# Expert stages with slot tiles of two 64-slot parts, the second part's weights copied by VectorE

## The chip, the cores and the metric

The kernel runs on one core of one Trainium2 chip. The metric is device microseconds of one launch; three runs of the kernel before took 2853.52, 2857.5 and 2858.4 us, median 2857.5 us. The engines are written as in the profile: PE is TensorE (PEld its weight loads), DVE is VectorE, ACT is ScalarE, POOL is GpSimd, SP is SyncE. A q behind a name (DVEq) is that engine's sequencer, which reads registers, waits on semaphores, branches and issues transfers.

## What is computed

One sequence of 1024 tokens with 512 features goes through six layers. Everything is float32. Each layer adds its result to x after a layer norm:

```
x = x + 0.5 * expert_ffn(ln(x))     # expert stage f0
x = x + attention(ln(x))            # 32 heads, causal
x = x + 0.5 * expert_ffn(ln(x))     # expert stage f1, same weights
x = x + 0.5 * lora_ffn(ln(x))
x = x + mamba(ln(x))
x = x + 0.5 * lora_ffn(ln(x))
```

The change lies in the two expert stages:

```
logits = x @ W_gate + b_gate                     # 8 experts
_, top_idx = top_k(logits, 2)
y_all = relu(einsum('bsd,edh->bseh', x, W_e) + b_e)   # W_e: 8 x 512 x 512
y = take_along_axis(y_all, top_idx[..., None], axis=2).mean(axis=2)
```

Only the two chosen experts of each token are needed, so there are 2048 pairs of token and expert per stage.

## The kernel before, in words

`expert_ffn` is called twice, with the tag f0 (ahead of attention) and f1 (behind it). It sorts the 2048 pairs by expert into slots. A slot tile is 128 slots of one expert; an expert's number of pairs is rounded up to whole tiles, so 16 tiles are always needed (NS0) and 23 at most (NS). The steps are these.

- Routing. The layer norm, the gate and the two best experts of each token are found, then ranks within each expert, the number of tiles per expert (`nt`, lines 458 to 467), the slot of each pair (`pos`), and, by small bf16 matmuls (line 526), the token of each slot (`token`) and the expert of each tile (`of_i`, line 592).
- Tiles. `gather(s)` (line 547) is an indirect transfer on POOL's queue: it fetches the 128 token rows of tile s from DRAM into `xs`. `turn(s)` (line 181) transposes them on PE by four 128x128 transposes and copies the result to `xt` on ACT (line 564). `slot_tile(s)` first turns tile s + 1, then multiplies tile s: four matmuls of 128 rows, 128 columns and 512 moving columns into one PSUM bank (line 608). The moving operand is the expert's 512x512 weight in `w_all`, picked by a register (`ep` on PE, `ev` on DVE) that is loaded from `of_i` (lines 604, 605). In float32 each matmul appears in the trace as two passes with a weight load each. DVE adds the bias (line 616), ACT applies the ReLU and the factor (line 622), and ACT's queue stores the tile to `outs` (line 623).
- The last tiles. Tiles 0 to 15 stand in straight code. Tiles 16 and up stand in nested `If(n > s)` blocks (line 649), where n is the real number of tiles, read into registers of PE, DVE, ACT and SP. Instructions are ordered by a scheduler within a block of straight code, and are not moved out of an `If` block.
- Collecting. POOL gathers the two result rows of each token from `outs` (line 666), and DVE adds them to x (line 695). It waits until all tiles are stored.

The buffers that matter: `xs`, `xt` and `y` have 3 buffers each, rows of late tiles come from a pool of 4 (`more_rows`), and PSUM tiles rotate through 4 banks (`psml`).

In f0 the weights come from DRAM while routing runs: experts 0 to 3 at once, 4 and 5 behind the fourth row store, the biases and experts 6 and 7 behind the second gather (`hold` puts a small POOL memset ahead of a transfer, so that the transfer waits for POOL's queue). POOL also runs six preparing products of the attention weights in f0 (lines 793 and 818), each queued behind one of the gathers of tiles 11 and up.

Of the kernel before, what the change touches and what calls it, by code (L numbers as in the profile page):

```python
# [22 lines left out]
P = 128  # L23
S = 1024
D = 512
NT = S // P
KT = D // P
# [5 lines left out]
HG = 4  # L33

NE = 8
NS = 2 * S // P + NE - 1
NS0 = 2 * S // P
NE1 = 4
RANK = 8
# [37 lines left out]
def macaron_kernel(  # L77
# [23 lines left out]
    nc = tc.nc  # L101
# [48 lines left out]
    def queue_behind(ins, prev):  # L150

        tc.add_manual_dep(
            ins.ins,
            prev.ins.name,
            mybir.DependencyInfo(mybir.DependencyClass.NoSync, mybir.DependencyReason.DATA),
            reason="queue_behind",
        )
        return ins

    def hold(w):  # L160

        tc.keep_in_program_order(nc.gpsimd.memset(w, 0.0))
# [166 lines left out]
    def gate_steps(keep=store_rows, own=None):  # L329
        return (  # L330
            lambda t: normalize(t, keep, own=own),
            transpose_h,
            None,
            lambda t: narrow_by_columns(t, gate_w, NE),
            gates,
        )

    def expert_ffn(tag, meanwhile, behind_weights=lambda: None):
# [4 lines left out]

        with tc.tile_pool(name=f"{tag}wa", bufs=1) as wap, tc.tile_pool(
            name=f"{tag}r", bufs=1
        ) as rp, tc.tile_pool(name=f"{tag}m", bufs=4) as more_rows, tc.tile_pool(name=f"{tag}w", bufs=3) as wk:
            w_all = wap.tile([P, NE, KT, D], F32, tag="w_all", name="w_all")
            b_all = wap.tile([P, NE, D], F32, tag="b_all", name="b_all")

            def load_expert(e):  # L350
                return nc.sync.dma_start(
                    w_all[:, e, :, :], w_e[e].rearrange("(k p) c -> p k c", p=P)
                )

            def load_biases():
                return nc.sync.dma_start(
                    b_all.rearrange("p e c -> p (e c)"),
                    b_e.rearrange("e c -> (e c)").partition_broadcast(P),
                )

            def gates_of_input():


                def keep(t, xn):
                    tc.keep_in_program_order(
                        nc.sync.dma_start(rows[t * P : (t + 1) * P, :], xn)
                    )
                    if t == 3:
                        for e in range(4, 6):
                            tc.keep_in_program_order(load_expert(e))  # L370

                def own(t):
                    return wk.tile([P, D], F32, tag=("xs", "xt", "y")[t % 3], name="xn_own")

                for e in range(4):
                    load_expert(e)
                Tiles(*gate_steps(keep, own)).flush()
# [8 lines left out]
            lanes = rp.tile([P, P], F32, tag="lanes", name="lanes")  # L386
            steps = rp.tile([P, NS + 1], F32, tag="steps", name="steps")
            counts = rp.tile([P, P], I32, tag="counts", name="counts")
            nc.gpsimd.iota(counts, pattern=[[1, P]], base=0, channel_multiplier=0)
            nc.gpsimd.tensor_copy(lanes, counts)  # L390
            nc.gpsimd.tensor_scalar(steps, lanes[:, : NS + 1], float(P), None, ALU.mult)

            over = rp.tile([P, NT], F32, tag="over", name="over")
            nc.gpsimd.tensor_copy(over, steps[:, :NT])
            nc.gpsimd.memset(over[:, 0:1], -1.0)
            bounds = rp.tile([P, NE + 1], F32, tag="bounds", name="bounds")
            nc.gpsimd.memset(bounds, 0.0)
# [12 lines left out]
            by_e = [P, NE, NT]  # L410
# [4 lines left out]
            if tag == "f0":  # L415
# [22 lines left out]
            ps = psml.tile([P, 512], F32, tag="ps", name="ps_rank")  # L438
            ne = NT * NE
# [5 lines left out]
                lhsT=ones_b,  # L445
                rhs=sums.rearrange("p e t -> p (e t)"),
                start=True,
                stop=False,
# [3 lines left out]
                lhsT=at_most_b,  # L452
                rhs=both.rearrange("p e t -> p (e t)"),
                start=False,
                stop=True,
            )
            more = rp.tile(by_e, F32, tag="more", name="more")
            nc.vector.tensor_tensor(
                more,
                ps[:, ne : ne + NE].unsqueeze(2).to_broadcast(by_e),  # L460
                over.unsqueeze(1).to_broadcast(by_e),
                ALU.is_gt,
            )
            nt = rp.tile([P, NE], F32, tag="nt", name="n_tiles")
            nc.vector.tensor_reduce(nt, more, AX.X, ALU.add)
            base, ends = bounds[:, :NE], bounds[:, 1:]
            nc.vector.tensor_tensor_scan(
# [3 lines left out]
            nc.vector.scalar_tensor_tensor(  # L471
                at,
                base.unsqueeze(1).to_broadcast([P, NT, NE]),
                float(P),
                ps[:, :ne].rearrange("p (e t) -> p t e", t=NT),
                ALU.mult,
                ALU.add,
# [11 lines left out]
            flat = pos.rearrange("p i t -> p (i t)")  # L489
            past = rp.tile([P, n2, NS + 1], BF16, tag="past", name="past_s")  # L490
            nc.vector.tensor_tensor(
                past,
                flat.unsqueeze(2).to_broadcast([P, n2, NS + 1]),
                steps.unsqueeze(1).to_broadcast([P, n2, NS + 1]),
                ALU.is_ge,
# [20 lines left out]
            ps = psml.tile([P, 512], F32, tag="ps", name="ps_slot")  # L516
            for j in range(n2):
                if j % 4 == 0:
# [48 lines left out]
            for s in range(2):  # L567
                gather(s)
            if tag == "f0":

                hold(b_all[0:1, :, 0:1])
                hold(w_all[0:1, 6:, 0, 0:1])
                tc.keep_in_program_order(load_biases())
                for e in range(6, NE):
                    tc.keep_in_program_order(load_expert(e))


            past = rp.tile([P, NS, NE], F32, tag="past_e", name="past")
            queue_behind(
                nc.vector.tensor_tensor(  # L580
                    past,
                    ends.unsqueeze(1).to_broadcast([P, NS, NE]),
                    lanes[:, :NS].unsqueeze(2).to_broadcast([P, NS, NE]),
                    ALU.is_le,
                ),
                known,
            )
            of = rp.tile([P, NS], F32, tag="of", name="of_f")
            nc.vector.tensor_reduce(of, past, AX.X, ALU.add)
            nc.vector.tensor_scalar(of, of, float(NE - 1), None, ALU.min)  # L590
            of_i = rp.tile([P, NS], I32, tag="of_i", name="of_i")
            nc.vector.tensor_copy(of_i, of)
            for i in range(2):
                queue_behind(nc.vector.tensor_copy(slot[i], pos[:, i, :]), known)
# [4 lines left out]
            def slot_tile(s):  # L599
                if s + 1 < NS:  # L600
                    turn(s + 1)
                xt = turned.pop(s)
                low, high = max(0, s - (NS - NE)), min(s, NE - 1)
                ep = nc.tensor.value_load(of_i[0:1, s : s + 1], min_val=low, max_val=high)
                ev = nc.vector.value_load(of_i[0:1, s : s + 1], min_val=low, max_val=high)
                ps = psml.tile([P, 512], F32, tag="ps", name="ps_e")
                for k in range(KT):
                    nc.tensor.matmul(
                        ps,
                        lhsT=xt[:, k, :],  # L610
                        rhs=w_all[:, bass.ds(ep, 1), k, :].rearrange("p e c -> p (e c)"),
                        start=(k == 0),
                        stop=(k == KT - 1),
                    )
                y = wk.tile([P, D], F32, tag="y", name="y_e")
                nc.vector.tensor_tensor(
                    y,
                    ps,
                    b_all[:, bass.ds(ev, 1), :].rearrange("p e c -> p (e c)"),
                    ALU.add,  # L620
                )
                nc.scalar.activation(y, y, AF.Relu, scale=0.25)
                nc.scalar.dma_start(outs[s * P : (s + 1) * P, :], y)

# [24 lines left out]
            with ExitStack() as more_tiles:  # L649
                n = nc.values_load(  # L650
                    n_i[0:1, :],
                    engines=[mybir.EngineType.PE, mybir.EngineType.DVE, mybir.EngineType.Activation, mybir.EngineType.SP],
                    min_val=NS0,
                    max_val=NS,
                )
                for s in range(NS0, NS):
                    more_tiles.enter_context(tc.If(n > s))
                    slot_tile(s)

    pairs = {}  # L660
# [910 lines left out]
    with tc.tile_pool(name="left", bufs=1) as left:  # L1571
        first, later = {}, []
# [67 lines left out]
```

## Time and profile before

| what | value |
|---|---|
| median of three runs | 2857.5 us |
| profiled execution: time, span | 2855.43 us, 2853.7 us |
| PE, DVE, ACT, POOL busy | 97%, 61%, 25%, 32% of the span |
| granted PE clock, mean | 0.984 |
| f0, from first to last expert matmul | 41.9 to 117.2 us |
| f1, from first to last expert matmul | 1597.0 to 1679.2 us |
| bias adds (line 616) | 40, of 692 ns |
| expert matmul passes (line 608) | 320, that is 40 tiles of 8 |

The profiled execution took 2855.43 us, of which 2853.7 us is the span from the first to the last instruction. The bias adds number 19 in f0 and 21 in f1. Within those two stretches PE was busy 75.14 of 75.20 us and 82.12 of 82.20 us, at a granted clock of 0.98 and 0.99. Behind each there is a stretch of some 13 us with almost no work on PE, in which the tiles' results are stored, gathered and added.

How to read it: a busy share over the whole span is an average over six layers with different limits, so a change in the expert stages is read from their own stretches. A row of the timeline gives start, duration, engine, line, operation, output and inputs, and in brackets the idle time ahead of it and what ended it. The group rows give total busy time and the mean duration of one.

### The profile page before, as it was taken

The page shows a single profiled execution, that of the slowest core. Times are in us where ns is not written, and L with a number is a line of the kernel's source. Part 1 is how long each engine was busy: PE and PEld are TensorE (multiplying, and loading weights), DVE is VectorE, ACT ScalarE, POOL GpSimd, SP SyncE. Part 2 cuts the span into 40 slices and gives each one's busy share as a digit, 9 for nine tenths or more (in the row PEclk, how much of TensorE's full clock was granted, in tenths as well). Part 3 has the DMA queues.
Part 4 walks back from the last instruction along what each step waited for, and adds up shares of the span by engine and source line. Part 5 has one row for each costly group of instructions (what it writes and reads, how often), then busy time and mean ns, then how long its engine had stood idle before and what let it go on. Part 6 is the DMA issues. An engine that isn't in the chain of part 4 may idle for free. (4 is left out here: it accounts for less than half of the span.)

```text
span 2853.7 us, 30231 instructions
## 1 busy us (share of the span) xinstructions
PE 2754.4 (97%) x11027; PEld 1565.0 (55%) x11027; DVE 1741.0 (61%) x3203; ACT 704.4 (25%) x1371; POOL 900.7 (32%) x751
## 2 busy tenths in 40 slices
PE   6799999999999999999999779999999999999998
PEld 3346566665666655666555435455555555555554
DVE  3356555565655656556555335877677776767673
ACT  2222222222221222212222224422223232222220
POOL 3512112121221222212200330455454545545450
PEclk8899999999999999999999889999999999999999
DMA  9511010010100101001014431323322322323210
GB/s 318 172 30 30 15 32 28 16 30 15 45 15 15 30 15 45 15 15 30 16 37 171 134 113 51 100 89 111 96 89 81 104 96 89 106 86 119 89 45 30
DMA packets 99605, 197.28 MB, mean 69 GB/s; under 512 B 8113, under 2 KB 33889, under 8 KB 99201
## 3 DMA queue, kind: packets, MB, share of 16 engines
q1 hardware_dynamic: 84944, 161.08, 17.3%
q0 software_dynamic: 6304, 20.47, 2.7%
q10 hardware_dynamic: 8208, 13.78, 1.3%
q8 instruction: 90, 1.47, 0.2%
q14 instruction: 59, 0.48, 0.1%
HBM read 176.17 MB, written 19.14 MB: 68 GB/s over the span
## 5 line engine op out<-in xcount | busy, mean ns | idle before, releaser
L867 PE MATMUL ps_s<-kT,qT 128*128 128x512 f32 (+3 forms) x768 | 292.8, 488 | 0.1
L891 PE MATMUL ps_o<-pT,v 128*128 128x512 f32 (+3 forms) x768 | 259.7, 488 | 0.0
L912 ACT COPY pT<-ps_tr 128x256 f32<-128x256 f32 (+2 forms) x192 | 91.5, 477 | 647.9 <-PE ps_tr L181 646.3
L881 ACT ACTIVATE pr<-ps_s,nm 128x128 f32<-128x128 f32 (+7 forms) x256 | 190.2, 743 | 238.7 <-DVE nm L878 208.4
L1530 PE MATMUL ps_out<-w_out,yg 128*128 128x512 f32 x512 | 238.5, 609 | 0.9 <-DVE yg L1493 0.9
L1460 POOL TENSOR_TENSOR cs<-cT,dd 128x1024 f32<-128x1024 f32 x56 | 182.5, 3259 | 177.8 <-PE ps_y L1478 136.9
L267 PE MATMUL ps_in<-hT,w_g 128*128 128x512 f32 x512 | 225.8, 594 | 1.1 <-ACT sg L1261 1.1
L267 PE MATMUL ps_in<-hT,w_x 128*128 128x512 f32 x512 | 225.5, 592 | 0.0
L891 PEld LDWEIGHTS ps_o<-pT,v 128*128 128x128 f32 x768 | 144.1, 191 | 145.1 <-issue 99.3
L878 DVE TENSOR_REDUCE nm<-ps_s 128x1 f32<-128x128 f32 (+7 forms) x256 | 192.5, 753 | 3.9
L181 PEld LDWEIGHTS ps_tr<-ident,pr 128*128 128x128 f32 x1152 | 136.6, 142 | 77.1 <-issue 44.9
L181 PE MATMUL ps_tr<-ident,pr 128*128 128x128 f32 x1152 | 171.1, 275 | 5.2 <-DVE pr L883 3.2
L883 DVE TENSOR_SCALAR pr<-pr,sm 128x128 f32<-128x128 f32 (+7 forms) x256 | 164.0, 641 | 7.4
L267 PEld LDWEIGHTS ps_in<-hT,w_x 128*128 128x128 f32 x512 | 97.1, 190 | 121.2 <-issue 120.8
L267 PEld LDWEIGHTS ps_in<-hT,w_g 128*128 128x128 f32 x512 | 96.6, 190 | 121.8 <-issue 119.8
L1433 DVE TENSOR_TENSOR_SCAN e_seg<-dd,eye 128x1024 f32<-128x1024 f32 x64 | 152.0, 2375 | 5.1 <-PE ps_y L1478 5.1
L1218 DVE SCALAR_TENSOR_TENSOR xc<-ps_in,conv,xc 128x511 f32<-128x511 f32 (+2 forms) x192 | 141.7, 738 | 20.8 <-ACT xc L1214 20.3
L867 PEld LDWEIGHTS ps_s<-kT,qT 128*128 128x128 f32 x768 | 127.5, 192 | 39.8 <-issue 26.8
L1530 PEld LDWEIGHTS ps_out<-w_out,yg 128*128 128x128 f32 x512 | 93.5, 193 | 95.3 <-issue 94.9
L965 POOL TENSOR_TENSOR so<-oT 128x256 f32<-128x256 f32 x28 | 20.0, 725 | 380.5 <-DVE oT L898 337.0
L818 POOL TENSOR_SCALAR w_q<-w_q 128x1024 f32<-128x1024 f32 x16 | 44.3, 2770 | 291.4 <-DMA w_q<-in_wq_dram 290.9
L1454 POOL TENSOR_TENSOR xw<-xdt,erev 128x512 f32<-128x512 f32 x56 | 59.3, 1060 | 229.6 <-DVE xdt L1448 190.8
(293 smaller groups left out, 4815.2 us busy)
## 6 DMA issues: line engine op xcount, KB each, us to landing
dd<-decay SPq DMA_DIRECT2D x128, 512.0 KB
w_all<-in_w_e_dram SPq DMA_DIRECT2D x16, 1024.0 KB
outs<-y_e ACTq DMA_DIRECT2D x40, 256.0 KB
w_v<-in_wkv_dram SPq DMA_DIRECT2D x8, 1024.0 KB
w_q<-in_wq_dram SPq DMA_DIRECT2D x32, 256.0 KB
w_k<-in_wkv_dram SPq DMA_DIRECT2D x8, 1024.0 KB
w_o<-in_wo_dram SPq DMA_DIRECT2D x8, 1024.0 KB
w_x<-in_in_wt_dram SPq DMA_DIRECT2D x8, 1024.0 KB
```

Of the source, the lines that this page charges most:

```text
L181: nc.tensor.transpose(ps[:, i * P : (i + 1) * P], src(i), ident)
L267: nc.tensor.matmul(ps[:, cols : cols + n], lhsT=w[:, k, c0 : c0 + P], rhs=hT[:, k, t0 : t0 + n], start=(k == 0), stop=(k == KT - 1),)
L867: nc.tensor.matmul(ps[:, j : j + m], lhsT=qT[:, qt * P : (qt + 1) * P], rhs=kT[:, j : j + m], start=True, stop=True,)
L878: nc.vector.tensor_reduce(nm, ps[:, :n], AX.X, ALU.max, negate=True)
L881: nc.scalar.activation(pr[:, :n], ps[:, :n], AF.Exp, bias=nm, accum_out=sm)
L883: nc.vector.tensor_scalar(pr[:, :n], pr[:, :n], sm, None, ALU.mult)
L891: nc.tensor.matmul(ps[:, lo:512], lhsT=v[:, kb, hh * P : (hh + 1) * P], rhs=pT[:, kb, lo:512], start=(kb == 0), stop=(kb == last),)
L912: nc.scalar.copy(dst, src)
L1218: in_line["conv"] = nc.vector.scalar_tensor_tensor(dst[:, s:], ps[:, : half - s], conv[:, ct, 3 - s : 4 - s], dst[:, s:], ALU.mult, ALU.add,)
L1433: segments = nc.vector.tensor_tensor_scan(e.rearrange("p h l -> p (h l)"), dd[:, 0, :], eye8.rearrange("p h l -> p (h l)"), 0.0, ALU.mult, ...
L1460: nc.gpsimd.tensor_tensor(cs, un["cT"][:, tok].unsqueeze(1).to_broadcast([P, HPG, P]), dd[:, 1, :].rearrange("p (h l) -> p h l", l=P), ALU ...
L1530: nc.tensor.matmul(po, lhsT=yg[:, k, :], rhs=w_o[:, k, :], start=(k == 0), stop=(k == 3))
```

## The change

A slot tile becomes two parts of 64 slots, and each part has its own expert. An expert's pairs are rounded up to whole parts of 64 instead of tiles of 128: at most 39 parts (NU), so at most 20 tiles (NS). The transposes of a tile stay as they are. Each of the four matmuls becomes two, of 64 columns each: the first part uses the left half of PE's columns and reads the weight in `w_all` by a register, as before; the second part uses the right half and reads `w2`, a 128x512 copy of the second expert's weight slice that DVE makes from `w_all` by its own register (pool `slices`, 5 buffers). The bias is added in two instructions of 64 partitions. The registers of DVE are two per tile. Tiles behind the sixteenth are in four `If` blocks instead of seven. The pool for late rows has one buffer instead of four.

In f0 the loads of experts 6 and 7 move from behind the second gather to behind the last row store; the biases keep their place.

```diff
-NS = 2 * S // P + NE - 1
+PARTS = 2
+U = P // PARTS
+NU = 2 * S // U + NE - 1
+NS = -(-NU // PARTS)
...
-                    if t == 3:
-                        for e in range(4, 6):
+                    if t % 4 == 3:
+                        for e in range(4 + t // 2 - 1, 4 + t // 2 + 1):
                             tc.keep_in_program_order(load_expert(e))
...
-            nc.gpsimd.tensor_copy(over, steps[:, :NT])
+            nc.gpsimd.tensor_scalar(over, lanes[:, :most], float(U), None, ALU.mult)
...
-                hold(w_all[0:1, 6:, 0, 0:1])
                 tc.keep_in_program_order(load_biases())
-                for e in range(6, NE):
-                    tc.keep_in_program_order(load_expert(e))
...
-                ep = nc.tensor.value_load(of_i[0:1, s : s + 1], min_val=low, max_val=high)
-                ev = nc.vector.value_load(of_i[0:1, s : s + 1], min_val=low, max_val=high)
+                ev = []
+                for u in range(s * PARTS, (s + 1) * PARTS):
+                    limits = dict(min_val=min(NE - 1, max(0, u - (NU - NE))), max_val=min(u, NE - 1))
+                    if u % PARTS == 0:
+                        ep = nc.tensor.value_load(of_i[0:1, u : u + 1], **limits)
+                    ev.append(nc.vector.value_load(of_i[0:1, u : u + 1], **limits))
                 ps = psml.tile([P, 512], F32, tag="ps", name="ps_e")
+                first, second = slice(0, U), slice(U, P)
                 for k in range(KT):
+                    w2 = slices.tile([P, D], F32, tag="w2", name="w_second")
+                    nc.vector.tensor_copy(
+                        w2, w_all[:, bass.ds(ev[1], 1), k, :].rearrange("p e c -> p (e c)")
+                    )
                     nc.tensor.matmul(
-                        ps,
-                        lhsT=xt[:, k, :],
+                        ps[first, :],
+                        lhsT=xt[:, k, first],
                         rhs=w_all[:, bass.ds(ep, 1), k, :].rearrange("p e c -> p (e c)"),
                         start=(k == 0),
                         stop=(k == KT - 1),
                     )
+                    nc.tensor.matmul(
+                        ps[second, :],
+                        lhsT=xt[:, k, second],
+                        rhs=w2,
+                        start=(k == 0),
+                        stop=(k == KT - 1),
+                    )
                 y = wk.tile([P, D], F32, tag="y", name="y_e")
-                nc.vector.tensor_tensor(
-                    y,
-                    ps,
-                    b_all[:, bass.ds(ev, 1), :].rearrange("p e c -> p (e c)"),
-                    ALU.add,
-                )
+                for i in range(PARTS):
+                    part = slice(i * U, (i + 1) * U)
+                    nc.vector.tensor_tensor(
+                        y[part, :],
+                        ps[part, :],
+                        b_all[part, bass.ds(ev[i], 1), :].rearrange("p e c -> p (e c)"),
+                        ALU.add,
+                    )
...
-                    min_val=NS0,
-                    max_val=NS,
+                    min_val=NS0 * PARTS,
+                    max_val=NU,
                 )
                 for s in range(NS0, NS):
-                    more_tiles.enter_context(tc.If(n > s))
+                    more_tiles.enter_context(tc.If(n > s * PARTS))
                     slot_tile(s)
```

More of the change, by code (lines that the diff above doesn't have):

```diff
@@ L345, in expert_ffn @@
             name=f"{tag}r", bufs=1
-        ) as rp, tc.tile_pool(name=f"{tag}m", bufs=4) as more_rows, tc.tile_pool(name=f"{tag}w", bufs=3) as wk:
+        ) as rp, tc.tile_pool(name=f"{tag}m", bufs=1) as more_rows, tc.tile_pool(name=f"{tag}s", bufs=5) as slices, tc.tile_pool(name=f"{tag}w", bufs=3) as wk:
             w_all = wap.tile([P, NE, KT, D], F32, tag="w_all", name="w_all")
@@ L391, in expert_ffn @@
             nc.gpsimd.tensor_scalar(steps, lanes[:, : NS + 1], float(P), None, ALU.mult)
-            over = rp.tile([P, NT], F32, tag="over", name="over")
-            nc.gpsimd.tensor_copy(over, steps[:, :NT])
+            most = S // U
+            over = rp.tile([P, most], F32, tag="over", name="over")
+            nc.gpsimd.tensor_scalar(over, lanes[:, :most], float(U), None, ALU.mult)
             nc.gpsimd.memset(over[:, 0:1], -1.0)
@@ L456, in expert_ffn @@
             )
-            more = rp.tile(by_e, F32, tag="more", name="more")
+            by_part = [P, NE, most]
+            more = rp.tile(by_part, F32, tag="more", name="more")
             nc.vector.tensor_tensor(
                 more,
-                ps[:, ne : ne + NE].unsqueeze(2).to_broadcast(by_e),
-                over.unsqueeze(1).to_broadcast(by_e),
+                ps[:, ne : ne + NE].unsqueeze(2).to_broadcast(by_part),
+                over.unsqueeze(1).to_broadcast(by_part),
                 ALU.is_gt,
             )
-            nt = rp.tile([P, NE], F32, tag="nt", name="n_tiles")
+            nt = rp.tile([P, NE], F32, tag="nt", name="n_parts")
             nc.vector.tensor_reduce(nt, more, AX.X, ALU.add)
@@ L473, in expert_ffn @@
                 base.unsqueeze(1).to_broadcast([P, NT, NE]),
-                float(P),
+                float(U),
                 ps[:, :ne].rearrange("p (e t) -> p t e", t=NT),
@@ L571, in expert_ffn @@
                 hold(b_all[0:1, :, 0:1])
-                hold(w_all[0:1, 6:, 0, 0:1])
                 tc.keep_in_program_order(load_biases())
-                for e in range(6, NE):
-                    tc.keep_in_program_order(load_expert(e))
-            past = rp.tile([P, NS, NE], F32, tag="past_e", name="past")
+            parts = NS * PARTS
+            past = rp.tile([P, parts, NE], F32, tag="past_e", name="past")
             queue_behind(
@@ L581, in expert_ffn @@
                     past,
-                    ends.unsqueeze(1).to_broadcast([P, NS, NE]),
-                    lanes[:, :NS].unsqueeze(2).to_broadcast([P, NS, NE]),
+                    ends.unsqueeze(1).to_broadcast([P, parts, NE]),
+                    lanes[:, :parts].unsqueeze(2).to_broadcast([P, parts, NE]),
                     ALU.is_le,
@@ L587, in expert_ffn @@
             )
-            of = rp.tile([P, NS], F32, tag="of", name="of_f")
+            of = rp.tile([P, parts], F32, tag="of", name="of_f")
             nc.vector.tensor_reduce(of, past, AX.X, ALU.add)
             nc.vector.tensor_scalar(of, of, float(NE - 1), None, ALU.min)
-            of_i = rp.tile([P, NS], I32, tag="of_i", name="of_i")
+            of_i = rp.tile([P, parts], I32, tag="of_i", name="of_i")
             nc.vector.tensor_copy(of_i, of)
@@ L602, in slot_tile @@
                 xt = turned.pop(s)
-                low, high = max(0, s - (NS - NE)), min(s, NE - 1)
-                ep = nc.tensor.value_load(of_i[0:1, s : s + 1], min_val=low, max_val=high)
-                ev = nc.vector.value_load(of_i[0:1, s : s + 1], min_val=low, max_val=high)
+                ev = []
[4 more added lines that the diff above has]
+                    ev.append(nc.vector.value_load(of_i[0:1, u : u + 1], **limits))
                 ps = psml.tile([P, 512], F32, tag="ps", name="ps_e")
+                first, second = slice(0, U), slice(U, P)
                 for k in range(KT):
+                    w2 = slices.tile([P, D], F32, tag="w2", name="w_second")
+                    nc.vector.tensor_copy(
+                        w2, w_all[:, bass.ds(ev[1], 1), k, :].rearrange("p e c -> p (e c)")
+                    )
                     nc.tensor.matmul(
-                        ps,
-                        lhsT=xt[:, k, :],
+                        ps[first, :],
+                        lhsT=xt[:, k, first],
                         rhs=w_all[:, bass.ds(ep, 1), k, :].rearrange("p e c -> p (e c)"),
```

## The prediction

> **What bounds the kernel now.** I read the busy rows of the page first, then the timeline of the expert stretches, then the rows of the operations that the change adds or moves.
>
> Page, parts 1 and 2:
>
> ```profile
> PE 2754.4 (97%) x11027; PEld 1565.0 (55%) x11027; DVE 1741.0 (61%) x3203; ACT 704.4 (25%) x1371; POOL 900.7 (32%) x751
> ...
> PE   6799999999999999999999779999999999999998
> ...
> PEclk8899999999999999999999889999999999999999
> ```
>
> PE carries the whole program; the low digits are the expert stages' edges. So PE time there counts in full. PE's timeline in two flagged tiles (those under `If`) of f0:
>
> ```profile
> 109.24 0.60 PE L181 MATMUL ps_tr<-ident,xs 128*128 128x128 f32 x4
> 109.67 3.60 PE L608 MATMUL ps_e<-w_all,xs 128*128 x8
> 113.11 0.60 PE L181 MATMUL ps_tr<-ident,xs_m 128*128 128x128 f32 x4
> ```
>
> From 109.24 to 113.11 one tile takes 3.87 us: 0.43 for the transposes, 3.44 for eight passes of 0.43. No gap, though these tiles stand behind a branch: before, DVE only comes in at the tile's end. DVE's timeline of the same stretch:
>
> ```profile
> 109.50 0.69 DVE L616 TENSOR_TENSOR y_e<-ps_e,b_all 128x512 f32<-128x512 f32 x1 [3.18 <-PE ps_e L608]
> 113.37 0.69 DVE L616 TENSOR_TENSOR y_e<-ps_e,b_all 128x512 f32<-128x512 f32 x1 [3.18 <-PE ps_e L608]
> ```
>
> DVE is free for 3.18 of 3.87 us.
>
> **What goes: three tiles.** Routing the reference's own inputs gives the pairs per expert: f0 248, 221, 241, 282, 295, 279, 237, 245 and f1 269, 225, 255, 258, 296, 258, 225, 262. In tiles of 128 that is 19 and 21, as the 40 bias adds confirm. In parts of 64 it is 35 and 37, so 18 and 19 tiles. 3 x 3.87 = -11.6 us. This is the whole gain; everything below is set against it.
>
> **The split matmuls.** Sixteen passes of 64 columns replace eight of 128. If halves run side by side, the time stays; if not, it doubles. PE's timeline has a neighbour of this form, the gate matmul of line 225, between full ones:
>
> ```profile
> 1548.97 0.60 PE L181 MATMUL ps_tr<-ident,ln_xn 128*128 128x128 f32 x4
> 1549.41 3.60 PE L926 MATMUL ps_wo<-w_o,oT 128*128 128x512 f32 x8
> 1552.94 0.66 PE L225 MATMUL ps_nc<-hT,gate_w 128*64 128x128 f32 x8
> 1553.53 0.66 PE L181 MATMUL ps_tr<-ident,ln_xn 128*128 128x128 f32 x4
> 1554.02 1.02 PE L926 MATMUL ps_wo<-w_o,oT 128*128 128x512 f32 x2
> ```
>
> Eight half passes of 128 moving columns take 0.59 us to the next start; full passes of this length follow at 0.109 us (four transposes in 0.44). Eight in sequence would be 0.87, four pairs 0.44. So halves do pair, with different moving data, and I take 0.43 us for a pair of 512 columns.
>
> The rest is the price of the mode. [...] The rows price it: the entry came 3.53 us after the eight full passes' start instead of 3.44 (0.09), the stretch took 0.59 instead of 0.44 (0.15), the transposes behind it 0.49 instead of 0.44 (0.05). Of the 0.15, about 0.05 is a weight load that 512-column passes hide. I take 0.24 us a tile: 37 tiles, +8.9 us. By a reading that nothing drains it is 0, by the rows unreduced 0.29 x 37 = 10.7.
>
> **The copies in the straight tiles.** Nearest row: line 1179, a float32 SBUF copy of 1024 elements in 695 ns; line 883 shows 478 ns for 512 and 753 for 1024 with one scalar more, so a copy of 512 is about 0.42 us. Per tile DVE does four copies (1.7) and two adds of 64 partitions (2 x 0.69, as long as one of 128): 3.1 us of a 4.1 us tile. In the changed kernel's order of instructions the copies of tile s + 2 stand between the adds of s and s + 1, and five buffers let them run five ahead. Cost 0 where nothing else is in the way. Two things are.
>
> Register reads: DVE reads `of_i` 32 times in the straight tiles instead of 16. The sequencer's rows of line 605 give 303 ns for the read, 183 for the address, 23 for the check, 0.65 with gaps. All 32 stand among the copies of the first eight tiles: three to five a tile add 2 to 3 us to 3.1, more than a tile, but the copies begin five ahead. I take 0, at most 2.
>
> [...] DVE and POOL in attention:
>
> ```profile
> 254.95 2.51 DVE L883 TENSOR_SCALAR pr<-pr,sm 128x640 f32<-128x640 f32 x1
> ```
> ```profile
> 254.65 2.46 POOL L793 TENSOR_TENSOR sqk<-w_k 128x1024 f32<-128x1024 f32 x1
> ```
>
> 640 elements take 0.55 us with POOL idle; this one ended as POOL's product did. [...] In f0, from 72.5 to 94.2 us, POOL runs six such products (15.0 us) and a gather per tile. By the products alone: one wait of half to a whole product (1.2 to 2.4) a tile makes DVE's tile 4.3 to 5.5 us against 4.1, so 1 to 8 us over six tiles, less some 2 of lead: 0 to 6, taken as +2. [...]
>
> **The flagged tiles: the dearest part.** No instruction is moved out of an `If`. So there the first copy comes behind: the last add of the tile before, the branch, two register reads. Behind the copy wait PE's second-half matmul, and behind that, in order, every later matmul. Counted from the last tile's end: 0.2 us until the add starts (the tile's row ends 113.11, add at 113.37), n_i read and branch 0.5 (first flagged tile only; branch alone 0.1), two reads 1.3, copy 0.42, hand-overs 0.2, and part of the second add (0.69) that the sequencer may have to wait for: 2.5 to 3.2. PE would have wanted the copy 0.54 after the tile's end (transposes, mode). Wait: 2.0 to 2.6 in the first, 1.6 to 2.3 later. With 2.3 and 2.0: f0 has two flagged tiles, f1 three: 4.3 + 6.3 = +10.6 us; bounds 7.5 and 13.
>
> **The tail.** The collecting waits for the last store. It now follows a second add: 0.69 x 2 = +1.4. In f1's order the ReLU of tile 17 stands behind the flag of 18, so its 0.63 and 0.33 of issue come last: +0.9 (0 to 1).
>
> **The rest.** Routing works on 21 and 20 columns instead of 24 and 23: six DVE operations about 0.05 shorter each, one of 64 elements longer: -0.3 in all. Experts 6 and 7 move ahead of the gathers on SP's queue, past nothing but the biases; all row stores still precede them. DMA was idle (share 0.00) from 34 to 36 us and had 0.51 in 30 to 32: 2 MB at 390 GB/s, 5.4 us, fill this up to about 36.6, beside the first gather (issued 34.80). PE's first matmul waits for the second gather (41.0), which then meets 2 MB less: 0, at most +1. The late-row pool of one buffer holds the one late tile: 0.
>
> **Sum.** -11.6 + 8.9 + 2 + 10.6 + 2.3 - 0.3 = +11.9 us. The profiled execution took 2855.4 us (2853.7 of span, 1.7 around it), so 2867.3; it lies 2.1 under the median, so **2869 us** for the median.
>
> **Rivals.**
> - Waits hidden (14%). DVE's sequencer reaches the flagged copies early, or long passes hide the drain: the flagged wait is 0.7 a tile (3.5) or the mode costs nothing. Either leaves +3 to +5: about 2861. For: the 0.24 is measured at 128 columns only. Against: reads, branch and adds are in one queue.
> - Faster half passes (6%). Two halves have two moving streams; if a pair of 512 takes less than one full pass, all 37 x 8 pairs gain: 127 us of pairs, so 10% is 12.7, and the change is faster than before once a pair is under 0.39 us. At 0.37 us: 2852. Against: pairs of 128 came at 0.109, just the full pass.
> - Lock with gathers (13%). [...]
> - Halves in sequence (3%). The change doesn't do what it says: 3.44 x 37 = +127, 2985 or more. Against: the gate row.
>
> **Chances.** My forecast has 64%, with an own range of 2864 to 2876. A measurement of this kernel tells about 0.2% (5.7 us) from no change. Faster by more: 0.06. Within: 0.14. Slower: 0.80. The range, 2858 to 2881, leaves out half of the second rival, the far end of the lock and the sequence.
>
> **What would show it.** Right: 18 and 19 tiles; starts 4.1 us apart in the straight tiles; line 617's copies at 0.42 us, some of 1.5 to 2.8 between 72 and 100 us; in flagged tiles an idle PE ahead of the second half, released by DVE, of about 2 us, five times; first-to-last matmul about 82 us in f0 (75.2 before) and 85 in f1 (82.2). Wrong: straight tiles at 3.9 us or under (the mode is free), flagged tiles without a gap, copies of 0.6 us or more, or DVE idle ahead of its copies everywhere.

## The result and the profile after

| | before | after |
|---|---|---|
| median of four runs each | 2856.54 us (2853.52 to 2858.4) | 2871.12 us (2869.96 to 2874.46) |
| ratio to before | 1 | 1.0057, 95% interval 1.0046 to 1.0069 |
| profiled execution: time, span | 2855.43, 2853.7 us | 2869.96, 2867.9 us |
| bias adds (two per tile after) | 40 | 74, that is 37 tiles |
| f0, third tile's transposes to the last expert pass's end | 70.05 us | 80.04 us |
| the same in f1 | 77.95 us | 81.21 us |

The change makes the kernel 14.6 us slower; 2869 was forecast. Three tiles are gone as expected, and what replaces them costs more than they did. The page after, parts 1 and 2:

```profile
PE 2761.9 (96%) x11287; PEld 1550.6 (54%) x11287; DVE 1836.4 (64%) x3385; ACT 704.2 (25%) x1365; POOL 895.3 (31%) x744
...
PE   6799999999999999999999779999999999999998
...
PEclk8999999999999999999999889999999999999999
```

The page hardly differs: 40 slices of 72 us are too coarse for a change in two stretches of 80 us. PE's busy time grew by only 7.5 us of the 14.2 in the span; the rest is idle PE. The two stretches by windows, f0 and f1, first before, then after with the stretch between them (start and end, length, then busy us of PE, PEld, DVE, ACT, POOL; then the granted clock, the DMA share and GB/s):

```profile
47.10:117.15 70.05, 70.05 (x217) 34.16 (x215) 12.45 (x18) 20.35 (x36) 29.40 (x20) 1.00 0.73 250
1601.18:1679.13 77.95, 77.94 (x242) 38.12 (x240) 13.84 (x20) 23.16 (x41) 15.46 (x16) 1.00 0.44 125
...
46.37:126.41 80.04, 76.59 (x342) 30.08 (x340) 61.20 (x98) 20.69 (x34) 29.95 (x20) 1.00 0.51 175
126.41:1610.28 1483.87, 1446.22 (x5468) 890.15 (x5468) 874.57 (x1816) 334.92 (x786) 293.47 (x266) 0.99 0.11 36
1610.28:1691.49 81.21, 78.52 (x363) 28.71 (x361) 52.06 (x104) 21.46 (x36) 14.20 (x14) 1.00 0.32 101
```

PE idles 3.45 us in f0 and 2.69 in f1, where it had idled for 0.0 before. A wait for a copy shows as idle only in part, since the first half's two passes run ahead alone for 1.07 us of it. DVE rose from 12.5 to 61.2 us in f0's stretch.

**Straight tiles.** PE's timeline of one tile in f0:

```profile
54.71 0.66 PE L185 MATMUL ps_tr<-ident,xs 128*128 128x128 f32 x4
55.30 0.64 PE L620 MATMUL ps_e<-w_all,xt_s 128*64 x1
55.30 0.64 PE L627 MATMUL ps_e<-w_second,xt_s 128*64 128x512 f32 x1
55.78 0.59 PE L620 MATMUL ps_e<-w_all,xt_s 128*64 x1
55.78 0.59 PE L627 MATMUL ps_e<-w_second,xt_s 128*64 128x512 f32 x1
...
58.35 0.59 PE L620 MATMUL ps_e<-w_all,xt_s 128*64 x1
58.36 0.59 PE L627 MATMUL ps_e<-w_second,xt_s 128*64 128x512 f32 x1
58.88 0.66 PE L185 MATMUL ps_tr<-ident,xs 128*128 128x128 f32 x4
```

The halves do run side by side: both passes of a pair begin within 0.01 us, and pairs follow at 0.43 us, as full passes did. The tile takes 58.88 - 54.71 = 4.17 us against 3.87. The additional 0.30 lies at the two edges: the last pair is followed by the transposes after 0.52 us and not 0.43; the four transposes to the first half take 0.59 and not 0.44; the first pair takes 0.48.

**Behind POOL's products.** DVE and POOL in f0, with the one PE row that waited:

```profile
79.94 1.39 DVE L637 TENSOR_TENSOR y_e<-ps_e,b_all 64x512 f32<-64x512 f32 x2 [0.23 <-issue]
80.87 1.07 POOL L553 DMA_INDIRECT xs<-rows,token  x1 [0.27 <-DMA outs<-y_e]
81.36 7.21 DVE L617 COPY w_second<-w_all 128x512 f32 x4
81.97 2.39 POOL L814 TENSOR_TENSOR sqk<-w_k 128x1024 f32<-128x1024 f32 x1
...
84.84 1.04 POOL L553 DMA_INDIRECT xs<-rows,token  x1 [0.48 <-PE ps_tr L185]
85.92 2.36 POOL L814 TENSOR_TENSOR sqk<-sqk,w_q 128x1024 f32<-128x1024 f32 x1
88.61 1.39 DVE L637 TENSOR_TENSOR y_e<-ps_e,b_all 64x512 f32<-64x512 f32 x2
88.63 1.07 PE L627 MATMUL ps_e<-w_second,xt_s 128*64 128x512 f32 x2 [0.48 <-DVE w_second L617]
```

Four copies take 7.21 us instead of 1.4. Two of them carry it: one begins at 81.36 and ends at 84.65, 0.29 us after the end of the product recorded from 81.97, that is from 0.61 us behind the copy's start; the next caught one begins at 85.24 and ends at 88.57, again 0.29 us after the product's end. The tile that ends here, at 89.63, takes 5.72 us, the two behind it 5.85 and 5.80, the next 4.45, and then 4.17 again: 5.1 us lost.

**Flagged tiles.** The first in f0, on three engines, with the start of the second:

```profile
114.07 0.66 PE L185 MATMUL ps_tr<-ident,xs 128*128 128x128 f32 x4
114.27 1.39 DVE L637 TENSOR_TENSOR y_e<-ps_e,b_all 64x512 f32<-64x512 f32 x2 [2.78 <-issue]
114.66 1.07 PE L620 MATMUL ps_e<-w_all,xs 128*64 x2
...
116.37 1.43 DVE L617 COPY w_second<-w_all 128x512 f32 x4 [0.70 <-DVE y_e L637]
116.85 0.64 PE L627 MATMUL ps_e<-w_second,xs 128*64 128x512 f32 x1 [1.12 <-DVE w_second L617]
...
120.42 0.66 PE L185 MATMUL ps_tr<-ident,xs 128*128 128x128 f32 x4
```

The first halves begin at 114.66, the second only at 116.85, once DVE has done two adds, the branch, the reads and a copy: 2.2 us late. The tile takes 6.35 us where it took 3.87. Measured so (second half's start less 0.59 from the transposes' start), the five waits are 2.18 and 1.74 us in f0, 2.55, 1.74 and 1.60 in f1: 9.8 in all.

**The tail.** DVE and ACT at f1's end:

```profile
1691.57 0.68 DVE L637 TENSOR_TENSOR y_e<-ps_e,b_all 64x512 f32<-64x512 f32 x1 [2.79 <-issue]
1692.62 1.30 DVE L637 TENSOR_TENSOR y_e<-ps_e,b_all 64x512 f32<-64x512 f32 x2 [0.36 <-DVEq L670]
1693.34 0.63 ACT L643 ACTIVATE y_e<-y_e 128x512 f32<-128x512 f32 x1 [6.42 <-DVE y_e L637]
...
1694.59 0.63 ACT L643 ACTIVATE y_e<-y_e 128x512 f32<-128x512 f32 x1 [0.61 <-ACT y_e L643]
```

Three adds follow the last pass: in the order of instructions the second add of tile 17 stands behind the whole block of tile 18, and its ReLU and store with it. From the last tile's first add to the next stage's first transposes it is 15.36 us in f1 (13.73 before) and 14.07 in f0 (13.06 before).

### The profile page after: what moved, and what is told of

Its sections match the earlier page's. It is cut to its first block, busy times and chain, and to the rows that moved or that the text cites. A ratio compares the mean times of both kernels' runs of the same rounds, so it can differ in the third digit from the quotient of the medians.

```text
span 2867.9 us, 31102 instructions
## 1 busy us (share of the span) xinstructions
PE 2761.9 (96%) x11287; PEld 1550.6 (54%) x11287; DVE 1836.4 (64%) x3385; ACT 704.2 (25%) x1365; POOL 895.3 (31%) x744
```

## The experiments

My theory was that of the prediction, with the sizes that the profile now showed: 0.30 us a tile for the change between full transposes and half matmuls, 5.1 us of lock in f0 (DVE's copies that end only behind POOL's product, 3.3 us instead of 0.43), 9.8 of waits for flagged copies. The rivals: all of it is DVE's pace, or the branch. The stretches of all runs, measured as in the table above (the middle column holds everything between them; of what the edits touch, only f0's tail and f1's first two tiles lie in it):

| kernel | ratio to before, 95% interval | f0 | between | f1 | span |
|---|---|---|---|---|---|
| before | 1 | 70.05 | 1484.03 | 77.95 | 2853.7 |
| changed | 1.0057 (1.0046 to 1.0069) | 80.04 | 1483.87 | 81.21 | 2867.9 |
| e8, changed again | 1.0062 (1.0048 to 1.0076) | 80.00 | 1487.69 | 81.21 | 2869.9 |
| e1, no copies | 0.9995 (0.9986 to 1.0004) | 70.98 | 1489.22 | 71.18 (18 tiles) | 2852.4 |
| e5, halves only | 1.0027 (1.0017 to 1.0038) | 75.57 | 1483.74 | 79.50 (20 tiles) | 2860.2 |
| e3, ACT copies | 1.0050 (1.0036 to 1.0064) | 74.91 | 1488.45 | 81.19 | 2866.3 |
| e4, 18 straight | 1.0030 (1.0019 to 1.0040) | 76.09 | 1484.09 | 77.37 | 2859.9 |
| e9, POOL when flagged | 1.0025 (1.0015 to 1.0035) | 76.06 | 1488.86 | 75.33 | 2860.2 |
| e6, pairs of turns | 1.0066 (1.0052 to 1.0080) | 80.46 | 1484.82 | 81.24 | 2868.2 |
| e7, all three | 0.9999 (0.9989 to 1.0008) | 69.40 | 1483.49 | 75.40 | 2850.1 |
| e10, mended | 0.9994 (0.9985 to 1.0004) | 71.26 | 1485.62 | 72.61 | 2852.4 |

**The changed kernel again, for the scatter (e8).**

> The changed kernel itself once more, beside the others on the same chip: ratio 1.0057 to the kernel before; its profile shows how far the stretches that the change does not touch (attention, f1's routing) differ from one profiled execution to the next, expected within 2 us, where the first profiles of five kernels spread over 4.8 us between f0 and f1.

Its f0 and f1 repeat within 0.04 us, but the code between them, the same in both, took 3.8 us longer, nearly all as busy PE (1450.10 against 1446.22 us). The granted clock tells where from: it stood at half for 37.6 us of this stretch in the first profile and for 47.8 us in e8, and PE was busy for 13.0 and 21.2 us of that time. 8.2 us more at half pace are about 4.1 us lost. The three profiles with the longest middle column (e1, e3, e9) each had 54.6 us at half. So single profiles decide within the two stretches, and the medians decide on the sum; the 2 us that I expected was too little.

**All copies away (e1).**

```diff
-                    w2 = slices.tile([P, D], F32, tag="w2", name="w_second")
-                    nc.vector.tensor_copy(
-                        w2, w_all[:, bass.ds(ev[1], 1), k, :].rearrange("p e c -> p (e c)")
-                    )
...
-                        rhs=w2,
+                        rhs=w_all[:, 0, k, :],
```

> The changed kernel without the copies: the second half of every tile reads expert 0's weights straight from w_all (part of the computation is left out: the second part's own weights). What stays is the mode price, the second bias add and the shorter tile count. Theory (waits come from the copies, the 0.30 us a tile from the change between full transposes and half matmuls): all straight tiles start 4.17 us apart, also where POOL runs its products, the flagged tiles too, and f0 and f1 lose 5.1 us of lock and 9.8 us of flagged waits against the changed kernel: 2871.1 - 14.9 = 2856 us. Rival A, the flagged gap comes from PE's own flag and register read: only the 5.1 go, 2866 us. Rival B, the 0.30 us a tile is DVE's pace with its copies and not the mode: tiles fall back to 3.87 us and another 11 us go, 2845 us.

Every tile from the third on is 4.17 us from the next, beside the products and under `If` alike (once in f1, 4.35, as in the changed kernel). f0 falls from 80.04 to 70.98 us: 9.06, which is the lock's 5.1 and the two flagged waits of 3.9. With other values out of f0, f1's routing came to 18 tiles instead of 19, so 4.17 of its 10.03 are a missing tile and 5.86 are the flagged waits. With that tile the median of 2853.4 us would be 2857.6, near the 2856 expected. Rival A (PE's own flag) and rival B (DVE's pace makes the 0.30) both fall.

**The mode alone, on the kernel before (e5).**

```diff
-                        ps,
-                        lhsT=xt[:, k, :],
+                        ps[:64, :],
+                        lhsT=xt[:, k, :64],
...
+                    nc.tensor.matmul(
+                        ps[64:, :],
+                        lhsT=xt[:, k, 64:],
+                        rhs=w_all[:, 0, k, :],
```

> The kernel before with its 128-slot tiles, each expert matmul split into two of 64 columns, the second half reading expert 0's weights straight from w_all (so the second half's own weights are left out, and f1's routing may come out with another number of tiles); no copies, one bias add. Theory: each tile costs 0.30 us more for the change between full and half matmuls, straight and flagged alike: 4.17 us from tile to tile everywhere, and with 40 tiles +12.0 us on the kernel before (3.87 us for each tile more or fewer). Rival, the first run without copies hides something that the part tiles bring: another price than 0.30.

From the fifth tile on, tiles are 4.17 us apart again (once in f1, 4.34), without copies, parts or second adds. f1 came to 20 tiles: 39 x 0.30 - 3.87 = +7.8 us expected, 2862.57 - 2854.47 = 8.1 measured. The 0.30 is a price of halves next to full transposes.

**Half as many changes of mode (e6).**

```diff
-                if s + 1 < NS:
-                    turn(s + 1)
+                if s == 0 or s % 2 == 1:
+                    for i in range(s + 1, min(s + 1 + (s > 0) + 1, NS)):
+                        turn(i)
...
-                for i in range(s + 2, NS if s == NS0 - 2 else min(s + 3, NS)):
-                    if i not in gathered and i > 1:
+                for i in range(s + 2, NS if s == NS0 - 2 else min(s + 5, NS)):
+                    if i not in issued:
```

> The changed kernel with two tiles turned together ahead of every second tile (gathers issued up to four tiles ahead), so that TensorE changes between full transposes and half matmuls half as often. Theory (0.30 us is the price of one change there and back): an even tile without transposes takes 3.43 us, an odd one 4.61, 8.04 for two against 8.34; seven such pairs in the straight code of each stage give -4.2 us, and nothing in the flagged tiles, where the wait for the copy covers it: 2867 us by the changed kernel's 2871. Rival A, the price lies in the half passes or their weight loads and not in the change: two tiles still take 8.34, no gain. Rival B, the earlier gathers come too late or hold up POOL's products: new waits of PE on DMA, slower.

PE's timeline in f1, one double tile:

```profile
1651.57 1.09 PE L185 MATMUL ps_tr<-ident,xs 128*128 128x128 f32 x8
1652.59 0.64 PE L621 MATMUL ps_e<-w_all,xt_s 128*64 x1
1652.60 0.64 PE L628 MATMUL ps_e<-w_second,xt_s 128*64 128x512 f32 x1
...
1659.61 1.09 PE L185 MATMUL ps_tr<-ident,xs 128*128 128x128 f32 x8
```

Two tiles take 1659.61 - 1651.57 = 8.04 us, as expected, against 8.34: the price goes with the number of changes, so it is the change itself, and rival A falls. But the whole came out no faster, and here I was wrong. The saving was eaten by waits that it did not touch or made longer: PE waited for gathered rows at f0's start (0.58 and 0.69 us, rival B), POOL's products cost 2.84 and 3.30 us on two double tiles, 1 us more than before, and in the flagged tiles the transposes no longer lay under the wait for the copy. On top of it f1's last tile ran slower behind its wait. PE's rows of that tile:

```profile
1687.08 0.64 PE L628 MATMUL ps_e<-w_second,xs 128*64 128x512 f32 x1 [2.02 <-DVE w_second L618]
...
1687.56 0.88 PE L628 MATMUL ps_e<-w_second,xs 128*64 128x512 f32 x1
...
1688.23 1.06 PE L628 MATMUL ps_e<-w_second,xs 128*64 128x512 f32 x1
...
1689.08 1.06 PE L628 MATMUL ps_e<-w_second,xs 128*64 128x512 f32 x1
```

From 1687.56 to 1690.79 the passes come 0.67 to 0.86 us apart and not 0.43; and the granted clock (third column from the end) says why:

```profile
1687.40:1690.80 3.40, 3.40 (x11) 1.58 (x9) 0.63 (x2) 0.00 (x0) 0.00 (x0) 0.55 0.02 5
```

**The lock taken away (e3).** If the copies are late because they run on DVE beside POOL's products, on ACT the 5.1 us go: 2871.1 - 5.1 = 2866 us, with tiles 10 to 13 at 4.17 us. A register of ACT, and in f0's tiles 9 to 13:

```diff
+                by_act = tag == "f0" and 9 <= s <= 13
...
+                    if by_act:
+                        nc.scalar.copy(
+                            w2, w_all[:, bass.ds(ea, 1), k, :].rearrange("p e c -> p (e c)")
+                        )
+                    else:
```

> The changed kernel with the copies of f0's tiles 9 to 13 on ACT instead of DVE; everything else is the same. [...] Rival A, the copies are slow there because of transfers or memory contention: ACT's copies are as slow, 2871 us. Rival B, ACT has 3.6 us of copying, evictions and ReLUs in a tile of 4.17 and becomes late itself: between 2866 and 2871, with waits on ACT.

All straight tiles of f0 are 4.17 us apart, and f0 lost 5.13 us. Number, then min, median and max in ns of the copies in f0, by engine:

```profile
L625 DVE COPY w_second<-w_all x47: 407/427/1247, 43.2 to 118.6; 128x512 f32 x47
L621 ACT COPY w_second<-w_all x20: 601/618/620, 76.1 to 96.1; 128x512 f32 x20
```

ACT's twenty copies ran beside the same products at 618 ns, none later than 620, so memory contention (rival A) and ACT's pace (rival B) both fall. The whole gained less than the 5.1: 2868.05 us, while its profile shows the stretch between 4.6 us longer. This goes with the clock: 54.6 us of that stretch were at half against 37.6, and all five runs of e3 had a mean granted clock of 0.981 or 0.982, where the nine runs of the changed kernel (e8's included) had 0.982 to 0.984. Whether the edit had a part in the lower clock stays open.

**The flagged waits, in two ways (e4 and e9).** First 18 straight tiles instead of 16; then copies on POOL, only under `If`.

```diff
-NS0 = 2 * S // P
+NS0 = 2 * S // P + 2
...
-                    min_val=NS0 * PARTS,
+                    min_val=2 * S // U,
```

> The changed kernel with 18 tiles in straight code instead of 16, so that f0 has no flagged tile and f1 one. Theory (the flagged wait is the copy that can't be issued ahead of its If block): the waits of 2.18 + 1.74 in f0 and 2.55 + 1.74 in f1 go, and f1's tile 18 becomes a first flagged tile, 2.5 instead of 1.6: 2871.1 - 8.2 + 0.9 = 2863.8 us. Rival, the copies would be late there anyway, because DVE's copies and adds fill the tile: 2871 us with the same gaps.

f0 fell by 3.95 us, f1 by 3.84, together 7.8 of the 7.3 expected, and the ratio from 1.0057 to 1.0030. The tiles freed of the flag are 4.17 us apart.

```diff
+                by_pool = s >= NS0
...
+                    if u % PARTS == 1 and by_pool:
+                        eg = nc.gpsimd.value_load(of_i[0:1, u : u + 1], **limits)
...
+                    if by_pool:
+                        nc.gpsimd.tensor_copy(
+                            w2, w_all[:, bass.ds(eg, 1), k, :].rearrange("p e c -> p (e c)")
+                        )
```

> The changed kernel with the copies of the tiles under If on POOL instead of DVE, POOL reading the flag and the register itself; 16 straight tiles as before. Theory (the wait in the flagged tiles is DVE's queue: last adds, branch, reads, then the copy): POOL has nothing queued there, makes its copies as buffers come free, and the waits of 3.9 us in f0 and 5.9 in f1 go, less what POOL's slower copy costs: with some 0.6 to 1.2 us a copy, four take 2.4 to 4.8 in a tile of 4.17, at most 0.6 a tile or 3 in all. So -7 to -10 by the changed kernel's ratio 1.006: 2862 to 2865 us. Rival, the wait is the branch itself, or the slices' buffers, whichever engine copies: no gain, 2871 us. [...]

POOL also reads the number of tiles, so it has the same branch ahead of its copies. f0 fell by 3.98 us and f1 by 5.88: 9.86, the whole of the 9.8. The first flagged tile of f1:

```profile
1673.36 0.62 POOL L621 COPY w_second<-w_all 128x512 f32 x1 [0.24 <-PE ps_e L635]
...
1674.05 0.66 PE L185 MATMUL ps_tr<-ident,xs 128*128 128x128 f32 x4
1674.22 0.62 POOL L621 COPY w_second<-w_all 128x512 f32 x1 [0.25 <-PE ps_e L635]
1674.25 1.39 DVE L645 TENSOR_TENSOR y_e<-ps_e,b_all 64x512 f32<-64x512 f32 x2 [2.78 <-issue]
...
1674.63 0.64 PE L628 MATMUL ps_e<-w_all,xs 128*64 x1
...
1674.64 0.64 PE L635 MATMUL ps_e<-w_second,xs 128*64 128x512 f32 x1
```

POOL makes its copies while the tile before still runs, since neither adds nor the reads of DVE stand ahead of them, and the two halves start together at 1674.63. So neither the branch nor the buffers made the wait; it was DVE's queue. DVE's adds beside POOL's copies still take 1.39 us for two, so POOL did not delay them.

**Together.** e7 has e3, e4 and e6; e10 has e3, e6 and e9, which need no knowledge of the number of tiles.

> The changed kernel with the three edits together: transposes of two tiles together, 18 tiles in straight code, f0's tiles 9 to 13 copied by ACT. By the theory the terms add: mode 17 x 0.15 x 2 = -5.1, flagged waits -7.3, lock -5.1, together 17.5 us off the changed kernel's 2871: 2853.5, some 3 us under the kernel before. Rival, one bound hides behind another (DVE's or ACT's pace, the gathers): part of it comes back as waits elsewhere, 2857 to 2863 us.

> The changed kernel with three mends that hold for any routing: flagged copies on POOL, f0's tiles 9 to 13 copied by ACT, transposes of two tiles together. By the theory the terms add: flagged waits -7 to -9.8, lock -5.1 (6 us in the kernel with pairs of transposes), mode 0.30 for every second tile, 8 or 9 a stage, -5: 17 to 20 us off 1.006, so 2852 to 2855 us, ratio 0.999 to 1.000. Rival, as in the first combination, the saved time comes back in the edges of the stage (tail with two adds, cold TensorE): 2857 or more.

e7's stretches fell by 10.64 and 5.81 us, e10's by 8.78 and 8.60. With most waits gone, the pairs of turns pay in f1: 2.72 us in e10 (against e9) and 1.97 in e7 (against e4). In f0 they pay 1.6 us in e7 and nothing in e10, where 71.26 us stand against 70.93 by e9 and e3 added up: PE waited there for gathered rows for 1.06 us and at another place for 0.62. At 2854.05 and 2853.74 us, beside 2854.47 and 2855.19 for the kernel before, both undo the loss, and neither can be told from the kernel before. The stretches with their tails come to -0.2 (e7) and -0.8 us (e10) against the kernel before, in line with that. The "cold TensorE" of e10's rival, the clock at half behind the stages, is there in any case: in the traces before and after it stood at half for 17.1 us behind f0 and again behind f1 (from 120.54 and 1683.84 before, from 129.70 and 1696.42 after). So there is no version here that beats it clearly: three tiles of 11.6 us pay for half of the mode changes (5.5 us by the 0.30), the longer tails and what waits are left.

## Why the prediction was right, and where its sizes were off

| term | forecast | measured | by |
|---|---|---|---|
| three tiles of 3.87 us | -11.6 | -11.6 | 74 adds, 37 tiles |
| change of mode, 37 tiles | +8.9 | +11.1 (0.30 each) | e1, e5, e6 |
| lock behind POOL's products | +2 | +5.1 | e3, e1 |
| register reads | 0 | 0 | straight tiles outside the lock at 4.17 |
| flagged waits | +10.6 | +9.8 | e9, e4 |
| tails | +2.3 | +2.6 | rows of both stages |
| routing, loads of experts 6 and 7 | -0.3 | under the scatter | |
| sum | +11.9 | +17.0 in stretches and tails; +14.2 in the profiled span, +14.6 between the medians | |

The direction and the order of the terms held: the flagged waits and the mode are each nearly as large as the gain. The terms sum to 2.8 us more than the span shows. Between the two first profiles, what lies outside came out some 2.5 us shorter after: 1.0 up to f0's third tile (begun 0.73 earlier though it had one change of mode behind it; routing and loads lie here), and 1.5 from the first transposes behind f0 to the first ones of f1. The second goes with the clock, which stood at half for 27.4 us of that stretch before and for 22.5 after. In e8, with 31.9, the stretch took 2.6 us more than in the first profile after, and e8's median lies 17.8 us over that of the kernel before beside it (2872.3 and 2854.47), as far as the terms say. That makes the hit on the median partly luck: a mode and a lock that were 5.3 us too small met runs that were favourable elsewhere. The stated range would have held 17.8 us too.

**The mode.** The step that was too small is "Of the 0.15, about 0.05 is a weight load that 512-column passes hide". It is not hidden: the first pair takes 0.48 us and not 0.43, and the transposes' row 0.66 instead of 0.60. In the trace after, the first weight load behind a change begins with its own pass (PEld and PE both at 58.88), where before it began 0.43 us ahead of it, beside the tile's last passes (112.68 and 113.11). That the time goes to this load is my reading. The rows unreduced, 0.29 x 37 = 10.7, which I gave as the upper bound, were nearly right. Whether PE drains at a change, as I took it, is not shown; the runs show 11.1 us for 37 tiles, a price that goes with the number of changes (e6).

**The lock.** The step that was too small is "one wait of half to a whole product a tile (1.2 to 2.4)". From 81 us on, a caught copy took 3.29 to 3.38 us in place of 0.43, in four of four cases. So it waited 2.9 us: it began 0.6 to 0.7 us ahead of the product's recorded start, while the gather ahead of it was still being issued, and ended 0.29 us behind the product. The row of attention had shown this last piece: DVE ended at 254.95 + 2.51 = 257.46, POOL's product at 257.11, not together. Then DVE's tile is two adds (1.39), three copies (1.0) and one of 3.3: 5.8 us, and this is just the spacing of the tiles there. The loss of 5.1 us lies within the 0 to 6 that the prediction gave for the products.

The prediction took all six products for alike, and they are not. The four that caught copies multiply two tensors (line 814, 793 before). The first two scale one tensor (line 839, 818 before):

```profile
73.02 2.38 DVE L617 COPY w_second<-w_all 128x512 f32 x4
73.41 2.89 POOL L839 TENSOR_SCALAR w_q<-w_q 128x1024 f32<-128x1024 f32 x1
75.77 1.39 DVE L637 TENSOR_TENSOR y_e<-ps_e,b_all 64x512 f32<-64x512 f32 x2 [0.36 <-issue]
```

All four copies end 0.9 us ahead of the product's end; the longest of them took 1.25 us. DVE even idled for 0.36 us ahead of its adds, so these products cost PE nothing, and the lead of the buffers was not needed for it.

Gathers held copies, but only a little. Copies of f1, where POOL issues gathers and no products (number, then min, median and max in ns):

```profile
L617 DVE COPY w_second<-w_all x76: 406/427/667, 1602.7 to 1688.4; 128x512 f32 x76
```

None of 76 took as long as a gather (1.01 us). The eleven over 0.44 us all began in the last 0.5 us of a gather and ended 0.23 us behind it, so a gather added at most 0.24 us to a copy, and no straight tile of f1 was late for it. So a product of line 814 held DVE's copies up to 0.29 us past its end, a product of line 839 until 1.56 us ahead of its end, and a gather until 0.23 us past its end. In the kernel before, line 199 had shown a like size: 512 elements took 606 ns with a gather beside them (at 132.95) and 545 without. No copy here waited for the whole of a gather, so the rival of 13% (a lock with gathers) falls.

**The flagged tiles.** From the first to the last expert matmul the stages take 85.1 and 85.7 us, forecast 82 and 85; f0's excess is lock and mode. For the waits the working held step by step: tile's end to second half 2.7 us in f0's first (forecast 2.5 to 3.2), and shorter later. (113.11, called the row's end there, is the start of the next transposes; the row ends at 113.27. Nothing in the sum hangs on it.)

**The other rivals.** Halves came side by side, at 0.43 us a pair and not faster, so neither the sequence nor the faster passes happened. No flagged copy came early.

## What to carry to other kernels

A finer tile that saves matmuls must be charged with what is fixed per tile, at its own edges: here 0.30 us for each change between full and half columns took back nearly the whole gain of 11.6 us, before any wait. Work that feeds PE behind a branch should sit on an engine with an empty queue: the same copies cost 9.8 us of PE on busy DVE, and nothing on POOL although POOL is slower (617 against 427 ns). And where a lock of another engine is longer than the lead that the buffers give, the engine's whole tile time is what PE sees, not the single wait: here 5.8 us a tile, with 2.9 of wait in it.

## What was not expected of the hardware

- A copy caught by POOL's product of two tensors ended 0.29 us after the product, four times within 0.01 us. The product of one tensor held copies for only a part of its time: a copy that began 0.08 us into it took 1.25 us and ended 1.56 us ahead of its end, both times. Of ACT's twenty copies of the same slices in e3 none was caught (601 to 620 ns), and in e9 DVE's adds from PSUM were not delayed by POOL's copies (1.39 us for two).
- In e6 PE idled for 2.0 us in a flagged tile of f1, and 3.4 us at half the granted clock followed (1687.73 to 1691.14), some 1.5 us of extra time (3.23 - 4 x 0.43) for the last tile. A longer idle stretch of the same run, 2.22 us up to 1675.40, was followed by passes at full pace, 0.43 us apart. In the traces before and after, all changes of the granted clock lie whole multiples of 3.41 us apart, within 0.01 us, so I count in steps of this length, in e6 from 1687.73. The 2.0 us then fall into one step, in which PE was busy for 1.39 us, and the 2.22 us are split over two, 0.90 and 1.32 us. In the traces before and after together, from the clock's first record on (11.31 and 13.65 us), each of the ten full-pace steps with PE busy for less than 1.40 us was followed by one at half, and none with more than 2.34; between these it went both ways, and what decides there is not shown.
- The same program took 3.8 us more over 1484 us of unchanged code in a second profile, as busier PE at half the clock (21.2 us against 13.0), not as waits. That the steps fall differently on the same instructions from one execution to the next would explain it, but is not shown. Near the end of attention a step of the changed kernel with PE busy for 1.56 us (1535.98 to 1539.40) was followed by one at half. No run here varies this on purpose.
